# Row sums of layer 2's attention: from a VectorE reduction to TensorE products with a column of ones

## The chip, the cores and the metric

The kernel runs on one core of one Trainium2 chip. The time is device microseconds of one execution; a kernel's time is the median of several executions. The profile is taken from one further execution, and all its times are microseconds from the start of its span unless marked otherwise. The engines are PE (TensorE; PEld are its weight loads), DVE (VectorE), ACT (ScalarE), POOL (GpSimd) and SP (which here only issues DMAs).

## The reference

The network has four layers on a float32 state x of 4 x 512 x 128. Each normalises x, computes an attention-like branch and a feed-forward branch from the result, and adds the product of the first with the silu of the second to x. Layer 0's branch is a selective scan; layers 1 to 3 have attention with 16 heads of 8 dimensions. The change touches the attention of layer 2, which differs from a softmax: the numerator uses rotated q and k, the denominator the plain ones.

```
att_num = exp(einsum('bhqd,bhkd->bhqk', q_rope, k_rope) * scale)
att_den = sum(exp(einsum('bhqd,bhkd->bhqk', q, k) * scale), axis=-1, keepdims=True)
att = att_num / att_den
y = einsum('bhqk,bhkd->bhqd', att, v)
```

So for each of 4 batches and 16 heads there are two 512 x 512 matrices of exponentials. Of the second only the sum over the keys is needed, one number for each query. The feed-forward branch of layer 2 is a mixture of 8 small experts (called moe2 below).

## The kernel before

**Tiling.** `attention(i, ...)` serves layers 1, 2 and 3. The work is cut into 16 groups, a batch and four heads each, and each group into four steps; a step k is one block of 128 rows for the four heads, taken in two halves (m = 0 and 1) of two heads. Layer 2 has 64 steps, one after the other.

**One step of layer 2** (`step`, with `ahead` = 0). For each half PE computes a first-pass product (`first_pass`, through `pair`, L878: two products of 48 x 128 with 48 x 512 in bf16 into a PSUM tile `wide` of 128 x 1024), ACT takes its exponential into `ep` (L980), and DVE sums `ep` over its 512 columns into `den` (L981). Here the queries stand on the partitions and the keys along the columns. Then, for the same half, PE computes a probability product from the rotated q and k, with the keys on the partitions (`probabilities`, L878 again), and ACT takes its exponential into `at` (L1016). Between the second first-pass product and the second probability product stands `behind(k)`: it calls `apply` for step k-1, in which PE multiplies the four heads' `at` with v (L1032): four float32 products of 128 x 32 with 128 x 512, each on its own strip of 32 columns of the array, all into one PSUM bank `py` and added up over the group's four steps.

**The end of a group.** After a group's fourth step ACT copies `py` to `osb` (L1038), and `finish` transposes it in four pieces on PE (L1049), takes the reciprocal of the sums on DVE (L1052) and multiplies (L1053). In layers 1 and 3 the sums come out of the product with v itself: the v tile `vaug` has 32 columns for each head, the first 8 hold v, column SUM = 8 holds ones, the rest zeros. In layer 2 the reciprocal reads `den`.

**Buffers.** `wide` has three PSUM tiles of two banks each, and the bank pools `bank` and `py` one bank each; these are all eight banks. `ep` has two buffers and `at` three. A tile that is written anew waits until all readers of the tile that held its buffer are done.

**The order.** All engines run their instructions in the order in which the program writes them (`tc.manual_schedule`), each engine in its own queue, with semaphores between them. Other work is put in by `Places`: `place()` is called once after the first half and once after the second half of each step and takes the next piece of the queued generators: the projections of the next batch (`project`: products on PE, `cos` and `qkr` for the rotation on POOL and DVE, casts into bf16 parts by `split`), `finish`, the row norms between the layers (`turn`, `post_rows`, `rows_norm`: statistics on DVE, L416 to L419, then a logarithm and an exponential on ACT, L422 and L423), and moe2. The side work on PE shares the one PSUM tile `bank`. In the last four steps of layer 2 the first pass of layer 3 runs too, whose scores DVE reduces (L985).

Of the kernel before, what the change touches and what calls it, by code (L numbers as in the profile page):

```python
# [11 lines left out]
F32 = mybir.dt.float32  # L12
BF16 = mybir.dt.bfloat16
I32 = mybir.dt.int32
AF = mybir.ActivationFunctionType
ALU = mybir.AluOpType
AX = mybir.AxisListType
# [3 lines left out]
P = 128  # L21
B, L, D = 4, 512, 128
# [7 lines left out]
SUM = HD  # L30


PARTS, FAR, SHIFT = 6, 6 * HD, 60
# [195 lines left out]
def kernel(ctx: ExitStack, tc: tile.TileContext, ap: dict):  # L229
    nc = tc.nc  # L230
    act, dve, pool, pe = nc.scalar, nc.vector, nc.gpsimd, nc.tensor
# [7 lines left out]
    def wide():  # L239
        return psum["wide"].tile([P, 2, 512], F32, tag="wide", name="wide")  # L240

    def bank(tag="bank"):
        tag = tag if psum["split"] else "bank"
        return psum["one"].tile([P, 512], F32, tag=tag, name=tag, bufs=psum["bufs"].get(tag, 2))
# [29 lines left out]
    def const(name):  # L274
        at, n = _CST[name]
        return cst[:, at : at + n]

    def col(name, i=0):
        at, _ = _COLS[name]
        return cols[:, at + i : at + i + 1]  # L280

    def row(name, n=4):
        r = _ROWS[name]
        return rows[:, r : r + 1, :].to_broadcast([P, n, D])
# [556 lines left out]
    def attention(i, hp, lp, xnT, pads, vaug, s_io, done=lambda b: None):  # L841
# [16 lines left out]
        if i == 2:  # L858
            kinds = ("q", "k", "qr", "kr")
            rope = lp.tile([P, 2, L], F32, name="rope")  # L860
            nc.sync.dma_start(out=rope, in_=ap["c_rope"])
        if i == 3:
            qbs = hp.tile([P, 1], F32, name="qbs")
            dve.tensor_scalar(qbs, col("q_b"), QSCALE, None, ALU.mult)
# [6 lines left out]
        def pair(lhs, rhs, n, m, blk, lo, hi, rows, own):  # L871


            ps = wide()
            cs = slice(blk * P, (blk + 1) * P)
            for j in range(2):
                r = slice(64 * j, 64 * j + rows)
                pe.matmul(ps[:, j, lo:hi], lhs[m][r, cs], rhs[m][r, lo:hi], start=True, stop=not own)  # L878
            if own:
                h = 4 * groups[n][1] + 2 * m  # L880
                for j in range(2):
                    lhs_own, rhs_own = ident_bf, mask_bf if causal else diag_bf[:, h + j, :]
                    if own == "keys":
                        lhs_own, rhs_own = rhs_own, lhs_own
                    pe.matmul(ps[:, j, cs], lhs_own, rhs_own, start=False, stop=True)  # L885
            return ps
# [34 lines left out]
        def project(b):  # L921

            places.need((i - 1, b))
            ts = slice(b * L, (b + 1) * L)
            w = wide()
            for m in range(2):
                pe.matmul(w[:, m, :], wqk[:, m, :], xnT[:, ts], start=True, stop=True)  # L927
            t = hp.tile([P, 2, L], F32, tag="qk", name="qk")
            if i == 3:
                act.activation(t[:, 0, :], w[:, 0, :], AF.Identity, bias=qbs, scale=QSCALE)  # L930
                act.activation(t[:, 1, :], w[:, 1, :], AF.Identity, bias=col("k_b"))
            else:
                act.activation(t[:, 0, :], w[:, 0, :], AF.Identity, scale=QSCALE)
                act.copy(t[:, 1, :], w[:, 1, :])
            yield 1
            values(b)
            yield 1
            parts = []
            if i == 2:
                cos, sin = (rope[:, m : m + 1, :].to_broadcast([P, 2, L]) for m in range(2))  # L940
                c = lp.tile([P, 2, L], F32, tag="cos", name="cos")
                pool.tensor_tensor(c, t, cos, ALU.mult)
                w = wide()
                for m in range(2):
                    pe.matmul(w[:, m, :], const("rot"), t[:, m, :], start=True, stop=True)
                r = lp.tile([P, 2, L], F32, tag="qkr", name="qkr")
                dve.tensor_tensor(r, w, sin, ALU.mult)
                pool.tensor_tensor(r, r, c, ALU.add)
                parts.append((r, lp.tile([P, 2, PARTS, L], BF16, tag="rparts", name="rparts")))
                yield 1  # L950
            parts.insert(0, (t, hp.tile([P, 2, PARTS, L], BF16, tag="parts", name="parts")))
            dense[b] = {}
            for kk, (_, d) in zip((("q", "k"), ("qr", "kr")), parts):
                dense[b].update({k: d[:, m].rearrange("p s t -> p (s t)") for m, k in enumerate(kk)})
            splits = [split(t, d, b) for t, d in parts]
            for _ in range(3):
                for sp in splits:
                    next(sp)
                yield 0
# [10 lines left out]

        def first_pass(n, qc, m):

            s = st[n]
            hi = (qc + 1) * P if causal else L
            ps = pair(s["q"], s["k"], n, m, qc, 0, hi, SHIFT if i == 3 else FAR, i != 2)
            if i == 2:
                if qc == 0 and m == 0:
                    s["den"] = lp.tile([P, 4, 4], F32, tag="den", name="den", bufs=3)
                e = lp.tile([P, 2, L], F32, tag="ep", name="ep", bufs=2)
                act.activation(e, ps, AF.Exp)  # L980
                dve.tensor_reduce(s["den"][:, qc, 2 * m : 2 * m + 2], e, AX.X, ALU.add)  # L981
            else:
                if qc == 0 and m == 0:
                    s["nm"] = hp.tile([P, 4, 4], F32, tag="nm", name="nm", bufs=2)
                dve.tensor_reduce(s["nm"][:, qc, 2 * m : 2 * m + 2], ps[:, :, :hi], AX.X, ALU.max, negate=True)  # L985
# [38 lines left out]
        def apply(n, kc):  # L1024
            b, g = groups[n]
            s = st[n]
            if kc == 0:
                s["po"] = bank("py")
            lo = kc * P if causal else 0
            a = s.pop(kc)  # L1030
            for j in range(4):
                pe.matmul(  # L1032
                    s["po"][32 * j : 32 * j + 32, lo:], vaug[b % 2][:, kc, 4 * g + j, :], a[:, j, lo:],
                    start=kc == 0, stop=kc == 3,
                )
            if kc == 3:
                s["osb"] = hp.tile([P, L], F32, tag="osb", name="osb", bufs=2)
                act.copy(s["osb"], s["po"])  # L1038

        def finish(n):  # L1040

            b, g = groups[n]
            s = st[n]
            if g == 0:
                outs[b] = hp.tile([P, 4, D], F32, tag="o", name="o")
            o = outs[b]
            pt = bank()
            for c in range(4):
                pe.transpose(pt[:, c * P : (c + 1) * P], s["osb"][:, c * P : (c + 1) * P], ident)  # L1049
            pv4 = pt.rearrange("p (c j r) -> p c j r", c=4, r=32)  # L1050
            rs = hp.tile([P, 4, 4], F32, tag="rs", name="rs", bufs=2)
            dve.reciprocal(rs, s["den"] if i == 2 else pv4[:, :, :, SUM])  # L1052
            dve.tensor_tensor(  # L1053
                o[:, :, g * 32 : (g + 1) * 32].rearrange("p c (j d) -> p c j d", d=HD),
                pv4[:, :, :, :HD],
                rs[:, :, :, None].to_broadcast([P, 4, 4, HD]),
                ALU.mult,
            )
            s.clear()
            yield 1  # L1060
            if g < NG - 1:
                return
            o = outs.pop(b)
            oT = hp.tile([P, L], F32, tag="osb", name="oT", bufs=2)
            transpose_chunks(oT, o, 4)
            yield 1
            pp = bank()
            for c in range(4):
                pe.matmul(pp[:, c * P : (c + 1) * P], oT[:, c * P : (c + 1) * P], wvo[:, 1, :], start=True, stop=True)
            ppv = pp.rearrange("p (c d) -> p c d", d=D)  # L1070
            sb = s_io[:, 4 * b : 4 * b + 4, :]
            dve.tensor_tensor(sb, ppv, row("out_b3") if i == 3 else sb, ALU.add)
            if i == 1:
                pool.tensor_tensor(sb, sb, row("b_proj1"), ALU.add)
            done(b)
            yield 1
# [21 lines left out]
        def behind(k):  # L1098

            if k > 0 and k not in through:  # L1100
                through.add(k)
                apply((k - 1) // 4, (k - 1) % 4)
                if k % 4 == 0:
                    places.job(1, finish(k // 4 - 1))
# [539 lines left out]
    s = keep.tile([P, NC, D], F32, name="s")  # L1644
# [8 lines left out]
    with banks("l1", 3, True, bank=1, py=1), tc.tile_pool(name="heads", bufs=1) as hp:  # L1653
# [34 lines left out]
        with ExitStack() as to3, tc.manual_schedule(engines=engines):  # L1688
# [28 lines left out]
            lp = to3.enter_context(tc.tile_pool(name="attn2", bufs=1))  # L1717
# [77 lines left out]
```

## Time and profile before

| what | us |
|---|---|
| three runs | 1807.21, 1817.28, 1823.47; median 1817.28 |
| the profiled execution | 1814.22, its span 1812.5 |
| PE busy | 1373.3 (76%) |
| DVE busy | 1143.7 (63%) |
| ACT busy | 955.1 (53%) |
| POOL busy | 536.2 (30%) |
| mean granted TensorE clock | 0.828 of full speed |
| first and last start of the reduction L981 | 991.8 and 1376.7 |

The page gives busy times over the whole span, in which four layers with different limits follow one another; the first and last start of L981 bound the stretch of layer 2's attention. A line of a group reads: source line, engine, operation, output<-input with shapes, count | busy us, mean ns of one | idle us of the engine just before them, and what ended it. A line of the waits reads: engine and what waited <- what it waited for: us in total, times, longest. A line of the timeline reads: start, duration, engine, line, operation. A line of the busy times by stage reads: stretch, its length, busy us (and instructions) of the engines, the granted TensorE clock, the DMA share and GB/s. One product in float32 leaves two records on PE, so a set of four v products has eight.

### The profile page before, as it was taken

The numbers are of one execution on the slowest core, as the hardware profiler recorded it, in microseconds if no ns is written. First come the engines' busy times: TensorE is split into PE (matmuls) and PEld (weight loads), VectorE is DVE, ScalarE is ACT, GpSimd is POOL, SyncE is SP. The second block draws the span as 40 slices with busy tenths as digits, with TensorE's granted clock in tenths as the row PEclk, the third lists the DMA queues.
The fourth block names the chain that finished last, engine by engine and source line by source line (L and its number), as shares of the span: only waits on it lengthen the run. The fifth ranks groups of instructions, "written<-read, shape, count | busy, mean of one in ns | idle before, by whom it ended". The sixth has DMA issues, their size and how long they took to land.

```text
span 1812.5 us, 22587 instructions
## 1 busy us (share of the span) xinstructions
PE 1373.3 (76%) x7845; PEld 699.2 (39%) x7845; DVE 1143.7 (63%) x1987; ACT 955.1 (53%) x1302; POOL 536.2 (30%) x513
## 2 busy tenths in 40 slices
PE   4678878788857888999586667776767877788771
PEld 2445445445532336888232222222312322233331
DVE  6467677677766664222466775657658799876422
ACT  3555655555524654223335777777885545354640
POOL 1245354444514652111534221214010101031223
PEclk8689889898857878999677877778868898598985
DMA  4557677576321231441302231220310211112112
GB/s 125 144 160 196 157 211 193 141 209 179 99 56 35 44 101 50 142 158 39 72 18 51 39 51 23 40 31 13 58 24 13 86 27 19 18 31 65 45 44 75
DMA packets 119122, 148.64 MB, mean 82 GB/s; under 512 B 15384, under 2 KB 79968, under 8 KB 117216
## 3 DMA queue, kind: packets, MB, share of 16 engines
q1 hardware_dynamic: 112048, 122.55, 28.7%
q0 software_dynamic: 6960, 24.65, 4.0%
q8 instruction: 62, 1.02, 0.2%
q14 instruction: 52, 0.43, 0.1%
HBM read 113.84 MB, written 16.01 MB: 72 GB/s over the span
## 4 chain that ended last, share of the span: by engine, by line
PE 43%; DVE 20%; ACT 15%; issue 10%; DMA 6%; POOL 3%; SPq 1%; POOLq 0%; DVEq 0%; ACTq 0%
PE wide L878 6%; PE py L1032 6%; PE wide L1313 5%; PE bank L562 5%; ACT at L1016 4%; PE py L573 4%; PE wide L885 3%; DMA rep<-ddd 3%; DVE nm L985 3%; PE py L1293 3%; ACT ep L980 3%; DVE den L981 2%; DVE hs L707 2%; PE wide L927 1%; ACT dA L696 1%
## 5 line engine op out<-in xcount | busy, mean ns | idle before, releaser
L1016 ACT ACTIVATE at<-wide 128x1024 f32<-128x1024 f32 (+3 forms) x384 | 352.5, 923 | 265.1 <-PE wide L885 175.6
L985 DVE TENSOR_REDUCE nm<-wide 128x2 f32<-128x1024 f32 (+3 forms) x256 | 256.8, 1019 | 105.1 <-PE wide L885 88.7
L1032 PE MATMUL py<-at,vaug 128*32 128x512 f32 (+3 forms) x1536 | 235.8, 671 | 11.7 <-POOL at L1020 8.5
L709 POOL TENSOR_TENSOR hc<-hs,C 128x512 f32<-128x512 f32 x128 | 163.2, 1279 | 250.3 <-DVE hs L707 145.1
L981 DVE TENSOR_REDUCE den<-ep 128x2 f32<-128x1024 f32 x128 | 155.5, 1217 | 115.0 <-ACT ep L980 114.3
L878 PE MATMUL wide<-k,q 48*128 48x512 bf16 (+4 forms) x768 | 167.9, 413 | 78.1 <-ACT at L1016 42.3
L562 PE MATMUL bank<-xnT,w 128*128 128x512 f32 x256 | 149.3, 738 | 75.7 <-ACT h L563 56.9
L980 ACT ACTIVATE ep<-wide 128x1024 f32<-128x1024 f32 x128 | 132.7, 1037 | 43.5 <-PE wide L878 33.9
L707 DVE TENSOR_TENSOR_SCAN hs<-dA,dBx 128x512 f32<-128x512 f32 x128 | 154.7, 1209 | 0.6 <-POOL hc L709 0.6
L573 PE MATMUL py<-w,h 128*128 128x128 f32 x1024 | 129.5, 288 | 19.6 <-DVE acc L523 19.6
L573 PEld LDWEIGHTS py<-w,h 128*128 128x128 f32 x1024 | 127.3, 204 | 38.6 <-DVE acc L523 27.9
L885 PE MATMUL wide<-own_bf 128*128 128x128 bf16 x880 | 138.8, 245 | 0.0
L696 ACT ACTIVATE dA<-rep,A 128x512 f32<-128x512 f32 x128 | 87.3, 715 | 97.6 <-DVE hs L707 69.4
L878 PE MATMUL wide<-q,k 63*128 63x512 bf16 (+3 forms) x512 | 101.9, 393 | 40.3 <-DVE nm L985 16.2
L703 DVE TENSOR_TENSOR dBx<-B,rep 128x512 f32<-128x512 f32 x128 | 89.0, 696 | 55.5 <-DMA rep<-ddd 35.8
L562 PEld LDWEIGHTS bank<-xnT,w 128*128 128x128 f32 x256 | 58.0, 237 | 166.6 <-ACT h L563 77.5
L878 PEld LDWEIGHTS <-q 48*128 48x128 bf16 (+1 forms) x768 | 49.8, 96 | 163.1 <-issue 145.3
L1313 PE MATMUL wide<-xT,w 128*128 128x256 f32 x456 | 108.5, 387 | 2.1 <-ACT h L1316 1.5
L1318 DVE TENSOR_TENSOR h<-h,wide 128x512 f32<-128x512 f32 x57 | 39.2, 688 | 110.5 <-ACT h L1316 110.5
L563 ACT ACTIVATE h<-bank,cols 128x512 f32<-128x512 f32 x128 | 84.7, 687 | 42.6 <-PE bank L562 42.2
L885 PEld LDWEIGHTS <-own_bf 128*128 128x128 bf16 x880 | 52.2, 101 | 113.8 <-issue 107.3
L878 PE MATMUL wide<-qr,kr 48*128 48x512 bf16 x256 | 61.3, 452 | 45.3 <-ACT ep L980 40.1
(324 smaller groups left out, 2086.7 us busy)
## 6 DMA issues: line engine op xcount, KB each, us to landing
rep<-ddd SPq DMA_DIRECT2D x256, 256.0 KB
q<-parts SPq DMA_DIRECT2D x192, 48.0 KB
k<-parts SPq DMA_DIRECT2D x192, 48.0 KB
w<-in_f_w_dram SPq DMA_DIRECT2D x18, 256.0 KB
ddd<-dd POOLq DMA_DIRECT2D x8, 512.0 KB
w<-in_f_w_dram SPq DMA_DIRECT2D x32, 128.0 KB
qr<-rparts SPq DMA_DIRECT2D x64, 48.0 KB
kr<-rparts SPq DMA_DIRECT2D x64, 48.0 KB
```

The source lines that it names most:

```text
L562: pe.matmul(ph, w1[:, f * P : (f + 1) * P], self.xnT[:, tb * L : (tb + 1) * L], start=True, stop=True)
L573: pe.matmul(py[:, cs], h[:, f, cs], w2[:, f, :], start=(f == 0), stop=(f == 3))
L707: dve.tensor_tensor_scan(h, st[n]["dA"], st[n]["dBx"], 0.0, ALU.mult, ALU.add)
L709: pool.tensor_tensor(hc, h, batch[tiles[n][0]]["C"], ALU.mult)
L878: pe.matmul(ps[:, j, lo:hi], lhs[m][r, cs], rhs[m][r, lo:hi], start=True, stop=not own)
L885: pe.matmul(ps[:, j, cs], lhs_own, rhs_own, start=False, stop=True)
L980: act.activation(e, ps, AF.Exp)
L981: dve.tensor_reduce(s["den"][:, qc, 2 * m : 2 * m + 2], e, AX.X, ALU.add)
L985: dve.tensor_reduce(s["nm"][:, qc, 2 * m : 2 * m + 2], ps[:, :, :hi], AX.X, ALU.max, negate=True)
L1016: act.activation(a[:, :, lo:], ps[:, :, lo:], AF.Exp)
L1032: pe.matmul(s["po"][32 * j : 32 * j + 32, lo:], vaug[b % 2][:, kc, 4 * g + j, :], a[:, j, lo:], start=kc == 0, stop=kc == 3,)
L1313: pe.matmul(ph[:, g, m * SLOT1 : (m + 1) * SLOT1], wk[:, f + g, m, :], self.x[k], start=True, stop=True)
```

## The change

The first pass of layer 2 swaps the roles of q and k, so the keys stand on the partitions of `ep` and the queries along its columns. The DVE reduction and the tile `den` go. `apply` gets four further products per step after those with v: the stationary operand is `ones`, a 128 x 32 float32 tile that is zero but for a column of ones at SUM + 1 = 9, the moving operand the first-pass exponentials of the same step. They add into the same bank `py`, in which row 9 of each head's 32 thus gathers the denominator over the four steps. `finish` reads the sums from column SUM + 1 of the transposed result. The exponentials live until the next step's `apply`, so `ep` has three buffers in place of two; the rotation's `cos` tile now shares these three buffers under the tag `ep` instead of having its own.

```diff
             rope = lp.tile([P, 2, L], F32, name="rope")
             nc.sync.dma_start(out=rope, in_=ap["c_rope"])
+
+            ones = lp.tile([P, 32], F32, name="ones")
+            dve.memset(ones, 0.0)
+            dve.memset(ones[:, SUM + 1 : SUM + 2], 1.0)
...
-                c = lp.tile([P, 2, L], F32, tag="cos", name="cos")
+                c = lp.tile([P, 2, L], F32, tag="ep", name="cos", bufs=3)
                 pool.tensor_tensor(c, t, cos, ALU.mult)
...
         def first_pass(n, qc, m):
             s = st[n]
             hi = (qc + 1) * P if causal else L
-            ps = pair(s["q"], s["k"], n, m, qc, 0, hi, SHIFT if i == 3 else FAR, i != 2)
             if i == 2:
-                if qc == 0 and m == 0:
-                    s["den"] = lp.tile([P, 4, 4], F32, tag="den", name="den", bufs=3)
-                e = lp.tile([P, 2, L], F32, tag="ep", name="ep", bufs=2)
-                act.activation(e, ps, AF.Exp)
-                dve.tensor_reduce(s["den"][:, qc, 2 * m : 2 * m + 2], e, AX.X, ALU.add)
+                ps = pair(s["k"], s["q"], n, m, qc, 0, L, FAR, False)
+                s["e", qc, m] = lp.tile([P, 2, L], F32, tag="ep", name="ep", bufs=3)
+                act.activation(s["e", qc, m], ps, AF.Exp)
             else:
+                ps = pair(s["q"], s["k"], n, m, qc, 0, hi, SHIFT if i == 3 else FAR, True)
...
             for j in range(4):
                 pe.matmul(
                     s["po"][32 * j : 32 * j + 32, lo:], vaug[b % 2][:, kc, 4 * g + j, :], a[:, j, lo:],
-                    start=kc == 0, stop=kc == 3,
+                    start=kc == 0, stop=kc == 3 and i != 2,
                 )
+            if i == 2:
+                for j in range(4):
+                    pe.matmul(
+                        s["po"][32 * j : 32 * j + 32, :], ones, s["e", kc, j // 2][:, j % 2, :], start=False, stop=kc == 3
+                    )
             if kc == 3:
                 s["osb"] = hp.tile([P, L], F32, tag="osb", name="osb", bufs=2)
                 act.copy(s["osb"], s["po"])
...
-            dve.reciprocal(rs, s["den"] if i == 2 else pv4[:, :, :, SUM])
+            dve.reciprocal(rs, pv4[:, :, :, SUM + (i == 2)])
```

## The prediction

> **What bounds the kernel now.** I read the page's busy table first: no engine fills the span (PE 76%, DVE 63%, ACT 53%), so the answer must come from the stage that the change touches. The groups of instructions place it: the first-pass reduction (L981) runs from 991.8 to 1376.7 us, so layer 2's attention is the stretch 990 to 1378, 64 steps in 388 us, 6.06 us a step. The groups of that stretch and its busy times by stage are next.
>
> ```profile
> L981 DVE TENSOR_REDUCE den<-ep 128x2 f32<-128x1024 f32 x128 | 155.5, 1217 | 115.0 <-ACT ep L980 114.3
> L1016 ACT ACTIVATE at<-wide 128x1024 f32<-128x1024 f32 x128 | 133.4, 1042 | 16.2 <-PE wide L878 15.9
> L1032 PE MATMUL py<-at,vaug 128*32 128x512 f32 x510 | 85.9, 750 | 0.0
> 990.00:1378.00 388.00, 279.69 (x1482) 100.34 (x1484) 265.94 (x438) 296.54 (x355) 80.92 (x53) 0.80 0.22 33
> ```
>
> In the last line (PE, PEld, DVE, ACT, POOL busy, then the granted clock) ACT leads with 296.5 of 388 us and idles 92; PE has 280, at a mean clock of 0.80. The waits of ACT in this stretch say what ends its idle time.
>
> ```profile
> ACT ep L980 <- PE wide L878: 33.9, 23, 7.4
> ACT r_r L422 <- DVE r_ve L419: 22.8, 9, 4.0
> ACT at L1016 <- PE wide L878: 15.9, 21, 1.4
> ACT ep L980 <- DVE den L981: 9.4, 3, 6.0
> ```
>
> The timeline shows an undisturbed step (start, duration) and then a set of v products at the lower clock.
>
> ```profile
> 1301.63 0.39 PE L878 MATMUL wide<-k,q 48*128 48x512 bf16 x2
> 1301.95 1.06 PE L1032 MATMUL py<-at,vaug 128*32 128x512 f32 x8
> 1302.94 0.39 PE L878 MATMUL wide<-qr,kr 48*128 48x512 bf16 x2
> 1303.12 1.11 ACT L980 ACTIVATE ep<-wide 128x1024 f32<-128x1024 f32 x1
> 1304.03 1.12 ACT L1016 ACTIVATE at<-wide 128x1024 f32<-128x1024 f32 x1
> 1304.93 1.13 ACT L980 ACTIVATE ep<-wide 128x1024 f32<-128x1024 f32 x1
> ...
> 1073.34 1.93 PE L1032 MATMUL py<-at,vaug 128*32 128x512 f32 x8
> ```
>
> ACT starts an exponential every 0.905 us (1303.12, 1304.03, 1304.93), so four make a step of 3.62 us; PE needs only about 2 us of it at full clock and waits. So ACT bounds the quiet steps, and the 92 us of holes lift the mean to 6.06. About 33 us of the holes wait on DVE directly. Another 24 us are PE's lateness where PE itself waited for DVE to empty the one PSUM bank that all side work shares: PE's waits on DVE results (L1452, L1460, L1422 and others) add up to 48 us.
>
> **What the change removes.** 128 reductions of 1.217 us, 155.5 us of DVE, which falls from 266 to 110 us in the stretch. Only what somebody waited for counts. (a) ACT waiting for the reduction to free an ep buffer: 9.4 us, all gone. (b) ACT waiting for the row statistics (r_ve), 22.8 us in nine waits. The reductions are queued ahead of them: at 1006.96 one ends, the statistics follow, and ACT gets r_ve at 1009.52. DVE without reductions runs ahead of ACT, but the statistics' own chain of about 2.2 us (four of 0.27 + 0.18, then 0.17), in half of the nine behind a POOL product of 1.28 and an addition of 0.68, remains. I take 15 back; the ends are 6 and 22.8. (c) Of the 24 us behind bank readers, the largest (7.40, ACT resuming at 1092.29) is PE behind the top-2 selection, in whose way two reductions stand and which started behind two more: 4 x 1.22 = 5 back. The 6.53 before 1146.08 is mostly DVE work of its own slowed beside POOL (casts of 1.4 and 1.6 against 0.68): 2.5 back. The waits before 1212.82, 1242.84, 1272.96 and 1110.37 have one or two reductions or statistics each in front: 8.5 back together. That is 16, with ends 5 and 24. Together 40 us, ends 20 and 56.
>
> **What it adds.** Each step gets four products of ones [128 x 32] with ep [128 x 512] in float32: the shapes and the dtype of the v products, on the same four column strips and the same PSUM bank, behind them. The v set starts its second half 0.45 us after the first and ends after 1.06, so a continued set costs 2 x 0.43 = 0.86 us, at the lower clock 1.72 (the set takes 1.93). The trace shows no such continued set. From below it is near nothing, if it filled strips idle during the v products (four strips are already busy, so I don't take it); from above a set by itself, 1.06 or 1.93. I take 0.86 and 1.72. That is 64 x 0.86 to 64 x 1.72, 55 to 110 us of PE, beside 108 idle.
>
> It would be hidden but for **the new wait**. ep has three buffers, and when the second first-pass exponential of step k is written (call it e1), the two of step k-1 and the first of step k are alive. So e1 must wait until the ones products of step k-1 have read theirs, and PE issues these after step k's second first-pass product and the v products. Behind e1 in ACT's queue stand the osb copy, the second probability exponential (a1) and the next step's, and PE's next v products wait for a1. In the step shown the v products end at 1303.01; ones to 1303.87; 0.07 for the signal (the osb copy starts 0.07 after the set that ends at 1281.44); e1 at 1303.94 in place of 1303.12: 0.82 lost, and since all that follows hangs on a1, lost in every such step (3.62 becomes 4.43). Where PE was behind (set 1127.53 to 1128.59, a1 at 1128.95) the ones end at 1129.45, e1 starts at 1129.52, a1 at 1130.43: 1.48. At the lower clock (1073.34 to 1075.27, a1 at 1075.86) a1 comes at 1075.27 + 1.72 + 0.07 + 0.905 = 1077.97: 2.1. I worked this out for all 63 steps from the set's end, with 0.47 for the osb copy where one stands between: 41 sets at full clock give 33 us, 22 at a lower one 45.
>
> Two corrections. Seven full-clock steps cost nothing only because e1 was late by DVE; that cover goes: +6. And eight of the 22 slow sets stand right behind PE pauses that DVE made, which go; PE also gets denser, so I let 12 turn full, at 2 us each: -24. **Price 60**, ends 33 + 6 = 39 and 78 + 6 = 84.
>
> The clock in the profile's rows by 8 us (PE busy, granted clock):
>
> ```profile
> 1056.00:1064.00 8.00, 5.06 (x24) 0.50 0.36 57
> 1304.00:1312.00 8.00, 6.75 (x46) 1.00 0.23 36
> ```
>
> The first follows a PE pause of 3.45 us and holds another of 2.64; the second is quiet steps. So PE's pauses cost a second time.
>
> The Trainium skill's page "TensorE: Matmul & The Clock Gate", Part 1, says that an idle window of about 3.4 us halves PE's clock and that about 3.4 us of sustained work restores it. It speaks for this change. The trace agrees in part: after a pause of 6.66 us a set at 1043.65 took 1.93 and the next, at 1047.56, 1.07; yet the half clock after 1052.92 lasted some 10 us. By the rule alone nearly all 22 would be full, which is the first rival.
>
> The smaller edits: cos now takes an ep buffer in three projections. POOL's two passes (2.35 and 2.36) hold it for some 5 us, in which e1 has one buffer less; it costs 0 where the wait on PE is longer anyway, at most 13 us if each of three costs two steps 2.2 us; I take 2. The role swap in the first pass keeps the shapes (48 x 128 held, 48 x 512 moved, 0.39 us). The reciprocal now reads PSUM behind the transposes that its neighbour L1053 already awaits, on an idle DVE: 0, at worst 16 x 0.24. Two memsets once: under 1. In the last four steps DVE also reduces layer 3's scores (1.22 each) and gets free: -2.
>
> **Sum**: -40 + 60 + 2 - 2 = +20 us. The profiled execution took 1814.22 us around a span of 1812.5; it becomes 1834. The median of the runs shown is 3 us higher, so I predict **1837**, 1.1% slower. About 1% (18 us) is what a measurement of this kernel can tell from no change.
>
> **Rivals.**
> 1. *The relief wins, faster.* PE without DVE's pauses keeps its full clock: then the 22 slow sets cost 0.1 each, the price is 33 + 6 + 2 + 2 = 43, the relief is near its upper end, 53, and some six waits of 1.38 us for half-clock products go as well, 8: -18, 1799. It decides once no more than about three of the 64 sets take over 1.9 us. For it: the quiet stretch at clock 1.00 has the least PE work per step. Against: half-clock stretches also follow ACT's own blocks (five us of table loads and Gelu before 1159.35) and thin products (L463, 3.74 us, then a set of 1.93).
> 2. *They cancel.* Relief 48, price 53: +5, 1822. Nothing in the profile excludes it; both terms are sums of small waits.
> 3. *The wait feeds itself.* e1 waits for PE, PE waits for the buffers that ACT frees, the clock stays low and cos blocks: price 84 + 13, relief 28: +69, 1886.
>
> That the reduction doesn't go is no case: there is no DVE instruction left for it. That e1 doesn't wait could only be if another buffer were free, and four live tiles on three exclude it.
>
> **How the numbers follow.** Forecast 0.42 (own range 1820 to 1862), relief 0.25, cancel 0.23, feeding itself 0.10. Range: the relief's end with 56 and the low price 39 (-17, and 3 for more waits gone) gives 1797; on the other side the high price 84 with relief 20 and 2 for cos less 2 gives +64, 1881; I take 1797 to 1878. Faster by over 1% (below 1799): two thirds of the first rival, 0.17. Within 1%: the rest of it, 0.08, the second, 0.23, and 0.04 of the forecast, 0.35. Slower: 0.48.
>
> **What would show it.** In the changed profile: no den group; L1032's neighbour of 512 records in the stretch with some 0.86 to 1.72 us per set; ACT's waits of ep on PE (ones) as the largest, 40 to 80 us, many of 0.5 to 1.5 us; r_ve down to some 8; steps of 4.4 us in quiet stretches; PE busy 340 or more. It is wrong if quiet steps stay at 3.6 (no wait), if the clock in the stretch is above 0.93 (first rival), or if the projections' steps stall on POOL (third).

## The result, and the profile after

The change made the kernel slightly faster: 1804.49 us (median of 20 runs, 1789.21 to 1816.35) against 1813.84 us for the kernel before (20 runs on the same chip). The ratio of the means, without the one slow run (1816.35 us), is 0.9935 with a 95% interval of 0.9915 to 0.9956. At 1814 us that is 12 us less (8 to 15; the medians themselves lie 9 apart), where 1837 us, 20 more than the median known then, was forecast. The time lies within the range given; the direction was wrong. It falls between two rivals: "they cancel" (+5) and "the relief wins" (-18).

The profiled execution of the changed kernel took 1797.64 us around a span of 1795.9 us, at a mean granted clock of 0.858 (before: 1814.22, 1812.5 and 0.828). From the first to the last start of an ep exponential, layer 2's attention took 384.9 us before and 372.0 us after, 12.9 us less. From there to the end of the span it is 437.1 us, against 436.8 before. The rest of the profile's difference, 4 us, lies ahead of the stage, where the two kernels have the same work. In the kernels run for this study the stage starts anywhere from 981 to 1001 us, so single profiles are compared below by the stage's own length, and kernels by such ratios to the kernel before, timed on the same chip.

The stretch's line in the busy times by stage (window, length, then PE, PEld, DVE, ACT, POOL busy, the granted clock, DMA share, GB/s), after the change:

```profile
986.50:1359.80 373.30, 308.35 (x1976) 109.95 (x1977) 129.84 (x310) 294.08 (x354) 83.47 (x53) 0.92 0.23 34
```

DVE falls from 266 to 130 us, as it had to. PE gets 504 records more (two a product, of 512) and yet only 30 us more busy time; the granted clock of the stage rose from 0.80 to 0.92. ACT's work is unchanged, 294 us, but PE, at 308 of 373 us, is now the busier of the two. The groups of that stretch, after:

```profile
L983 ACT ACTIVATE ep<-wide 128x1024 f32<-128x1024 f32 x128 | 131.5, 1028 | 71.8 <-PE py L1041 56.4 <-POOL qkr L952 9.4 <-PE wide L882 5.5
L1019 ACT ACTIVATE at<-wide 128x1024 f32<-128x1024 f32 x128 | 132.1, 1032 | 0.0
L1035 PE MATMUL py<-at,vaug 128*32 128x512 f32 x504 | 75.0, 670 | 0.0
L1041 PE MATMUL py<-ep,ones 128*32 128x512 f32 x504 | 72.8, 653 | 0.0
```

The v products (L1035) have a mean of 670 ns in place of 750: fewer of them run at the lower clock. Of the 64 sets of v products 11 took over 1.2 us, against 23 before. The ones products (L1041) cost almost as much PE time again. ACT's idle time, 79 us, now stands almost all before the first-pass exponential, as its waits show (total, times, longest):

```profile
ACT ep L983 <- PE py L1041: 56.4, 48, 3.9
ACT ep L983 <- POOL qkr L952: 9.4, 3, 3.2
ACT ep L983 <- PE wide L882: 5.5, 5, 2.3
ACT r_r L422 <- DVE r_ve L419: 1.6, 2, 1.3
```

The new wait is the largest one and is as large as forecast: 56 us in 48 of 63 steps. The old ones are gone: ep behind a late score product from 33.9 to 5.5, the row statistics from 22.8 to 1.6, the probability exponential behind PE from 15.9 to none listed, the reduction from 9.4 to none. So the stage exchanged one set of waits for another and came out ahead. The timeline of a step without other work shows the new wait as it was drawn up (start, duration; idle before and releaser in brackets):

```profile
1266.40 1.06 PE L1035 MATMUL py<-at,vaug 128*32 128x512 f32 x8
1267.28 1.04 PE L1041 MATMUL py<-ep,ones 128*32 128x512 f32 x8
1268.42 1.02 ACT L983 ACTIVATE ep<-wide 128x1024 f32<-128x1024 f32 x1 [1.55 <-PE py L1041]
1269.34 1.02 ACT L1019 ACTIVATE at<-wide 128x1024 f32<-128x1024 f32 x1
```

The ones set starts 0.88 us after the v set and ends at 1268.32; ACT's exponential, which needs the buffer that it reads, starts at 1268.42 after 1.55 us of nothing. Four quiet exponentials now take 4.33 us in place of 3.62.

### The profile page after: what moved, and what is told of

Its sections match the earlier page's. It is cut to its first block, busy times and chain, and to the rows that moved or that the text cites. A ratio compares the mean times of both kernels' runs of the same rounds, so it can differ in the third digit from the quotient of the medians.

```text
span 1795.9 us, 23471 instructions
## 1 busy us (share of the span) xinstructions
PE 1402.4 (78%) x8357; PEld 709.9 (40%) x8357; DVE 1006.8 (56%) x1861; ACT 954.2 (53%) x1302; POOL 538.8 (30%) x513
## 4 chain that ended last, share of the span: by engine, by line
PE 45%; ACT 15%; DVE 14%; issue 10%; DMA 9%; POOL 5%; SPq 2%; POOLq 0%; another core or an unknown queue 0%; ACTq 0%; DVEq 0%
PE py L1035 7%; PE wide L882 6%; PE wide L1321 6%; PE bank L562 5%; ACT at L1019 5%; DMA rep<-ddd 4%; PE py L573 3%; PE wide L889 3%; PE py L1301 3%; ACT ep L983 2%; DVE nm L988 2%; PE py L1041 2%; DVE hs L707 2%; PE wide L931 1%; DMA xs<-acc,pos 1%
## 5 line engine op out<-in xcount | busy, mean ns | idle before, releaser
L1035 PE MATMUL py<-at,vaug 128*32 128x512 f32 (+3 forms) x1536 | 227.0, 646 | 11.6 <-POOL at L1023 8.4
L882 PE MATMUL wide<-q,k 63*128 63x512 bf16 (+4 forms) x768 | 156.6, 395 | 52.2 <-ACT at L1019 32.0
L983 ACT ACTIVATE ep<-wide 128x1024 f32<-128x1024 f32 x128 | 131.5, 1028 | 71.8 <-PE py L1041 56.4
L882 PE MATMUL wide<-k,q 60*128 60x512 bf16 (+4 forms) x512 | 101.8, 383 | 70.6 <-ACT at L1019 34.3
L882 PEld LDWEIGHTS <-k 63*128 63x128 bf16 (+1 forms) x768 | 46.0, 94 | 208.4 <-issue 185.6
L1321 PEld LDWEIGHTS wide<-xT,w 128*128 128x128 f32 x456 | 83.4, 193 | 15.7 <-issue 3.4
L882 PE MATMUL wide<-qr,kr 48*128 48x512 bf16 x256 | 52.5, 402 | 32.0 <-ACT ep L983 29.6
```

What stands on the lines that cost most here:

```text
L983: act.activation(s["e", qc, m], ps, AF.Exp)
L1035: pe.matmul(s["po"][32 * j : 32 * j + 32, lo:], vaug[b % 2][:, kc, 4 * g + j, :], a[:, j, lo:], start=kc == 0, stop=kc == 3 and i != 2,)
L1321: pe.matmul(ph[:, g, m * SLOT1 : (m + 1) * SLOT1], wk[:, f + g, m, :], self.x[k], start=True, stop=True)
```

## The experiments

Two explanations fit a net of -12 us. **Theory A**: the price of the new wait was right (60) and the relief far larger than 40, some 75. **Theory B**: the relief was right and the price far smaller, some 28. A third, **C**, says that neither is a size of its own: relief and price meet in PE's lateness and in its clock. The "stage" below is the length from the first to the last start of an ep exponential in one profiled execution.

**The relief alone.** In the kernel before, the 128 reductions are taken out and a constant stands for the row sums; nothing is added on TensorE. The row sums are left out of the computation.

```diff
                 if qc == 0 and m == 0:
                     s["den"] = lp.tile([P, 4, 4], F32, tag="den", name="den", bufs=3)
+                    dve.memset(s["den"], 512.0)
...
-                dve.tensor_reduce(s["den"][:, qc, 2 * m : 2 * m + 2], e, AX.X, ALU.add)
```

> The kernel before without the 128 reductions (den is set to a constant once a group; the row sums are left out, nothing takes their place, ep keeps two buffers). It measures the relief alone. If the relief was mis-sized (theory A: DVE's queue cost the stage some 75 us, not the 40 of the prediction): 65 to 85 us faster than before, stage of layer 2 near 310 us, ACT's idle time in it near 15 us. If the price of the wait was mis-sized (theory B: the relief is 40 as predicted and the wait costs some 28 net): 35 to 45 us faster, stage near 345. If it is the clock that PE's extra products keep up (theory C): the granted clock of the stage stays near the 0.80 of before and the gain is at most 40; under theory A it rises to 0.88 or more without any added product.

Measured: 1768.87 us against 1813.43, ratio 0.9742 (0.9700 to 0.9783), or -47 us (39 to 54 less). Stage 330.3 us. Busy times of the stretch, and ACT's waits:

```profile
997.00:1328.50 331.50, 263.49 (x1470) 95.93 (x1470) 128.25 (x324) 291.50 (x353) 80.88 (x53) 0.86 0.25 39
```

```profile
ACT ep L981 <- PE wide L878: 17.7, 15, 6.0
ACT at L1016 <- PE wide L878: 9.3, 15, 1.3
ACT r_r L422 <- DVE den L979: 5.1, 1, 5.1
```

The relief is near the value predicted, 40, and within its ends, 20 to 56. A's 75 falls. The time and the clock of 0.86 lie between what was expected under A and under B and C. ACT is busy 291 of 331 us, and its waits for late score products are halved without any change to PE's own work. From here to the changed kernel it is +35 us (0.9742 to 0.9935): that is the price in a stage already relieved of the reductions.

**The price alone.** In the changed kernel the reductions are put back, unused, beside the ones products.

```diff
                 act.activation(s["e", qc, m], ps, AF.Exp)
+                if qc == 0 and m == 0:
+                    s["den"] = lp.tile([P, 4, 4], F32, tag="den", name="den", bufs=3)
+                dve.tensor_reduce(s["den"][:, qc, 2 * m : 2 * m + 2], s["e", qc, m], AX.X, ALU.add)
```

> The changed kernel with the 128 reductions kept beside the ones products (their result is read by nobody; nothing is left out). It measures the price without the relief. Theory A: against the changed kernel 50 to 75 us slower, so some 40 to 65 us slower than before. Theory B: 25 to 35 us slower than before. Theory C: the clock of the stage stays near the changed kernel's 0.92 although DVE is as loaded as before.

Measured: 1881.82 us against 1813.43, ratio 1.0370 (1.0330 to 1.0409), or +67 us (60 to 74). Stage 454.2 us.

```profile
990.00:1445.30 455.30, 340.01 (x1976) 117.06 (x1977) 265.30 (x436) 295.22 (x354) 80.92 (x53) 0.84 0.19 28
```

```profile
ACT ep L983 <- PE py L1044: 101.8, 47, 6.1
ACT r_r L422 <- DVE r_ve L419: 23.8, 9, 3.9
```

Here the price is near the 60 predicted, just above the 40 to 65 expected under A, and B's 28 falls as well. Beside a loaded DVE the same wait, in 47 steps, costs 101.8 us in place of 56.4, and the row statistics are as late as they were before. Removing the reductions is worth 47 us without the ones products and 79 us with them (1.0370 to 0.9935); adding the ones products costs 67 us with the reductions and 35 without. Both differences are 32 us. So the two terms of the sum aren't independent, and neither A nor B is right. Nor is C in the form expected here, that the added products alone hold the clock near 0.92: beside the reductions it is 0.84.

**The order on PE.** In each step the ones products are issued ahead of the v products, which depend on them for nothing but the bank.

```diff
-            for j in range(4):
-                pe.matmul(
-                    s["po"][32 * j : 32 * j + 32, lo:], vaug[b % 2][:, kc, 4 * g + j, :], a[:, j, lo:],
-                    start=kc == 0, stop=kc == 3 and i != 2,
-                )
             if i == 2:
                 for j in range(4):
                     pe.matmul(
-                        s["po"][32 * j : 32 * j + 32, :], ones, s["e", kc, j // 2][:, j % 2, :], start=False, stop=kc == 3
+                        s["po"][32 * j : 32 * j + 32, :], ones, s["e", kc, j // 2][:, j % 2, :], start=kc == 0, stop=False
                     )
+            for j in range(4):
+                pe.matmul(
+                    s["po"][32 * j : 32 * j + 32, lo:], vaug[b % 2][:, kc, 4 * g + j, :], a[:, j, lo:],
+                    start=kc == 0 and i != 2, stop=kc == 3,
+                )
```

> The changed kernel with the ones products issued before the v products of the same step, so that ep is read 0.86 us (full clock) or 1.72 us earlier while PE does the same work. If the wait of ep on the ones products costs the stage what its 56 us in the profile say, this wait falls to some 10 to 20 us, quiet steps go from 4.34 back to 3.6 to 3.8 us, and the time falls by 20 to 40 us against the changed kernel. If the wait only takes the place of holes that would be there anyway, the wait falls but the time by less than 10 us.

Measured: 1786.45 us against 1813.43, ratio 0.9836 (0.9797 to 0.9876), or -30 us. Stage 355.8 us, a quiet step 3.68 us.

```profile
ACT ep L983 <- PE py L1036: 25.3, 27, 3.9
```

The same products, with the same operands, on the same buffers: 18 us of the price came from their place behind the v products. The buffer is free as soon as the ones set ends, and no exponential waits for the v set to end any more. The wait falls from 56.4 to 25.3 us; what is left stands in other steps than the quiet ones. Both figures just miss what was expected, a wait of 10 to 20 us and a gain of 20 to 40.

**cos out of the ep buffers.** In the changed kernel the rotary product gets a tile of its own, worked in two halves so that it fits.

```diff
-                c = lp.tile([P, 2, L], F32, tag="ep", name="cos", bufs=3)
-                pool.tensor_tensor(c, t, cos, ALU.mult)
...
-                r = lp.tile([P, 2, L], F32, tag="qkr", name="qkr")
...
-                pool.tensor_tensor(r, r, c, ALU.add)
+                r = lp.tile([P, 2, L], F32, tag="qkr", name="qkr")
...
+                for m in range(2):
+                    c = lp.tile([P, L], F32, tag="cos", name="cos")
+                    pool.tensor_tensor(c, t[:, m, :], rope[:, 0, :], ALU.mult)
+                    pool.tensor_tensor(r[:, m, :], r[:, m, :], c, ALU.add)
```

> The changed kernel with cos in a small buffer of its own (two halves of 512 columns, one after the other), so that it takes none of the three ep buffers. The wait of ep on POOL (9.4 us in three waits) goes. If these waits stand on the path: 7 to 10 us faster than the changed kernel; if another wait is next (ep on the ones products): less than 4 us.

Measured: 1803.02 us against 1813.43, ratio 0.9944 (0.9915 to 0.9972), the same as the changed kernel within the intervals; stage 372.2 us against 372.0.

```profile
ACT ep L984 <- PE py L1042: 62.5, 46, 6.7
```

The 9.4 us that ACT waited for POOL are gone, and the wait for the ones products is 6.1 us longer. The sharing costs nothing that can be measured: the next wait was right behind it. The run also moves POOL's product behind DVE's, so it isn't the sharing alone.

**PE's time without the wait.** The ones products read a constant tile (`flat`, 128 x 512 ones, written once) in place of ep, so they take PE's time and make nobody wait; ep has two buffers, and cos its own, as in the kernel before. The row sums are left out of the computation.

```diff
-                c = lp.tile([P, 2, L], F32, tag="ep", name="cos", bufs=3)
+                c = lp.tile([P, 2, L], F32, tag="cos", name="cos")
...
-                s["e", qc, m] = lp.tile([P, 2, L], F32, tag="ep", name="ep", bufs=3)
-                act.activation(s["e", qc, m], ps, AF.Exp)
+                e = lp.tile([P, 2, L], F32, tag="ep", name="ep", bufs=2)
+                act.activation(e, ps, AF.Exp)
...
-                        s["po"][32 * j : 32 * j + 32, :], ones, s["e", kc, j // 2][:, j % 2, :], start=False, stop=kc == 3
+                        s["po"][32 * j : 32 * j + 32, :], ones, flat, start=False, stop=kc == 3
```

> The changed kernel in which the ones products read a constant tile of ones in place of the first-pass exponentials (the row sums are left out; every product is still issued, four float32 ones a step at the same place). ep then has no reader and two buffers, cos its own; so DVE is relieved and PE as loaded as in the changed kernel, but no exponential waits for the ones products. It divides the 36 us between the changed kernel and the one without any sums (1804.5 against 1768.9 us). If the price is the wait: within 8 us of 1769, quiet steps at 3.62, no wait of ep on PE's ones. If it is PE's time: 1790 to 1805. The prediction's price was all wait: by it about 1769. Clock of the stage: if the added products warm PE, at or above 0.92; if only the missing DVE pauses do, near the 0.86 of the kernel without sums.

Measured: 1783.29 us against 1813.69, ratio 0.9822 (0.9780 to 0.9863), or -32 us. Stage 348.9 us, quiet steps 3.61 to 3.70.

```profile
995.50:1345.60 350.10, 300.84 (x1962) 107.51 (x1966) 120.41 (x309) 293.92 (x353) 83.29 (x53) 0.92 0.25 37
```

```profile
ACT at L1021 <- PE wide L884: 25.8, 26, 2.6
ACT ep L985 <- PE wide L884: 14.1, 17, 3.4
```

The price of 35 us divides into about 15 for PE's time (0.9742 to 0.9822) and about 20 for the wait (0.9822 to 0.9935); the time lies between the two values expected, so neither is the whole. The time alone isn't free, although PE is idle 49 of 350 us here: score products come later, and ACT's waits for them rise from 27 to 40 us.

**The wait taken away by buffers.** The whole change is kept; ep and cos share five buffers in place of three, and at has two in place of three to make room.

```diff
-                c = lp.tile([P, 2, L], F32, tag="ep", name="cos", bufs=3)
+                c = lp.tile([P, 2, L], F32, tag="ep", name="cos", bufs=5)
...
-                s["e", qc, m] = lp.tile([P, 2, L], F32, tag="ep", name="ep", bufs=3)
+                s["e", qc, m] = lp.tile([P, 2, L], F32, tag="ep", name="ep", bufs=5)
...
-                s[kc] = hp.tile([P, 4, L], F32, tag="at", name="at", bufs=3)
+                s[kc] = hp.tile([P, 4, L], F32, tag="at", name="at", bufs=2)
```

> The changed kernel with five buffers for ep and cos together in place of three (at has two in place of three to make room; nothing is left out). With five, the second first-pass exponential of a step finds a free buffer without the ones products of the step before, also while cos holds one. If the wait is the price: quiet steps back at 3.62, time 1770 to 1780. If it is PE's time: 1790 to 1805, with other waits of ACT on PE in its place.

Measured: 1781.17 us against 1813.69, ratio 0.9811 (0.9765 to 0.9857), or -34 us, the same as with the constant tile and just over the 1770 to 1780 us expected for the wait; stage 345.1 us. The wait for the ones products is gone, and what is left is of the same kind and size as there:

```profile
ACT at L1019 <- PE wide L882: 22.7, 23, 2.6
```

With the row sums right, this shows by another way that the wait is worth some 20 us.

**PE's time without the wait, beside the reductions.** The same constant tile, and the reductions put back.

```diff
-                s["e", qc, m] = lp.tile([P, 2, L], F32, tag="ep", name="ep", bufs=3)
-                act.activation(s["e", qc, m], ps, AF.Exp)
+                e = lp.tile([P, 2, L], F32, tag="ep", name="ep", bufs=2)
+                act.activation(e, ps, AF.Exp)
+                if qc == 0 and m == 0:
+                    s["den"] = hp.tile([P, 4, 4], F32, tag="rs", name="den", bufs=2)
+                dve.tensor_reduce(s["den"][:, qc, 2 * m : 2 * m + 2], e, AX.X, ALU.add)
...
-                        s["po"][32 * j : 32 * j + 32, :], ones, s["e", kc, j // 2][:, j % 2, :], start=False, stop=kc == 3
+                        s["po"][32 * j : 32 * j + 32, :], ones, flat, start=False, stop=kc == 3
```

cos has its own tile here too. The output is divided by the constant tile's sums and the reductions' results go unused, so the row sums are left out again.

> The kernel with the ones products on a constant tile (no exponential waits for them) and the 128 reductions kept on DVE (neither gives the divisor used: the row sums are left out of the result). It divides the 68 us that the ones products cost beside the reductions (1881.8 against 1813.4) into PE's time and the wait. Without reductions PE's time cost 14 us and the wait 21. If PE's time is what grows under DVE's load (PE is late behind DVE, and each set adds to that): 35 to 60 us slower than before. If the wait grows (the products themselves hide in PE's pauses): 5 to 20 us slower than before, and the wait is worth some 50. By the prediction, which charged the wait alone and hid PE's time: no more than 5 us slower.

Measured: 1827.77 us, ratio 1.0143 (1.0111 to 1.0175) to the kernel before on the chip of this run (1801.21 us), or +26 us, between the two ranges expected and well over the 5 us that the prediction allows. The one profile shows a stage of 399.8 us, 15 more than before; but the profile of before is from a run of 1814 us, not 1801, so the stages aren't like for like.

```profile
981.40:1382.30 400.90, 317.37 (x1970) 109.93 (x1970) 264.03 (x436) 295.86 (x353) 80.93 (x53) 0.87 0.21 32
```

```profile
ACT at L1024 <- PE wide L884: 39.6, 30, 3.1
ACT ep L985 <- PE wide L884: 24.5, 21, 7.4
ACT r_r L422 <- DVE r_ve L419: 22.1, 9, 3.5
```

So beside the reductions PE's time costs about 26 us and the wait another 41 (1.0143 to 1.0370), against 15 and 20 without them. By the intervals given I estimate some 10 us of doubt on each such difference: that the wait costs more beside the reductions is just clear of it, that PE's time does is not. The six kernels in one table, in us against the kernel before (ratio less 1, times 1814):

| | no ones products | ones products, no wait | ones products and wait |
|---|---|---|---|
| without reductions | -47 | -32 | -12 (the change) |
| with reductions | 0 (before) | +26 | +67 |

Reading across a row gives the price, down a column the relief. Removing the reductions is worth 47, 58 and 79 us: the more PE has to do and the more ACT waits for it, the more a free DVE is worth.

**Cheaper ones products.** ep and the ones in bfloat16, otherwise as changed; the row sums then add rounded terms.

```diff
-            ones = lp.tile([P, 32], F32, name="ones")
+            ones = lp.tile([P, 32], BF16, name="ones")
...
-                s["e", qc, m] = lp.tile([P, 2, L], F32, tag="ep", name="ep", bufs=3)
+                s["e", qc, m] = lp.tile([P, 2, L], BF16, tag="ep", name="ep", bufs=3)
```

> The changed kernel with ep and ones in bf16 (the exponentials are rounded before they are summed; order and buffers as in the changed kernel). A bf16 product of 512 columns is one pass: pairs of first-pass products start 0.23 us apart at full clock, so the ones set should add about 0.22 us instead of 0.86, and 64 x 0.64 = 41 us less PE time. The wait shrinks by 0.64 us in a quiet step: 3.7 us a step. If wait and PE time are the whole price: 20 to 30 us faster than the changed kernel, near 1780. If ACT's write of bf16 or the weight loads bring something new: less than 10 us faster.

Measured: 1786.76 us against 1813.69, ratio 0.9855 (0.9810 to 0.9901), or -26 us; stage 352.1 us. The ones products' busy time falls from 72.8 to 28 us, and the wait for them from 56.4 to 35.1. That is 15 us under the changed kernel, less than the 20 to 30 expected: a cheaper ones set still stands behind the v set.

```profile
ACT ep L983 <- PE py L1041: 35.1, 28, 3.4
```

**Both, and ep with four buffers.** bfloat16 as above, the ones products first, and the freed memory used for a fourth ep buffer and a cos tile of its own.

```diff
-            ones = lp.tile([P, 32], F32, name="ones")
+            ones = lp.tile([P, 32], BF16, name="ones")
...
-                c = lp.tile([P, 2, L], F32, tag="ep", name="cos", bufs=3)
+                c = lp.tile([P, 2, L], F32, tag="cos", name="cos")
...
-                s["e", qc, m] = lp.tile([P, 2, L], F32, tag="ep", name="ep", bufs=3)
+                s["e", qc, m] = lp.tile([P, 2, L], BF16, tag="ep", name="ep", bufs=4)
...
-                        s["po"][32 * j : 32 * j + 32, :], ones, s["e", kc, j // 2][:, j % 2, :], start=False, stop=kc == 3
+                        s["po"][32 * j : 32 * j + 32, :], ones, s["e", kc, j // 2][:, j % 2, :], start=kc == 0, stop=False
```

The v products follow them, as in the run with the order turned round.

> All three together: ones products first and in bf16, ep with four bf16 buffers, cos with a buffer of its own. No wait of ep on PE, PE time of 0.22 us a step added. It should come to within 10 us of the kernel without sums, 1769 to 1779, and be faster than both kernels of this case. If it stays above 1785, some of the price is neither the wait nor PE's time.

Measured: 1758.71 us against 1813.69, ratio 0.9703 (0.9663 to 0.9743), or -54 us: 3.0% under the kernel before and, by the two ratios, 2.3% under the changed one. It is the fastest kernel here, faster than the 1769 to 1779 us expected, and as fast as the one that computes no row sums at all (0.9742, the intervals overlap). Its stretch, and one set in its timeline:

```profile
993.20:1333.10 339.90, 276.17 (x1720) 102.78 (x1722) 122.99 (x309) 292.43 (x353) 82.57 (x53) 0.86 0.25 38
```

```profile
1256.39 0.40 PE L1036 MATMUL py<-ep,ones 128*32 128x512 bf16 x4
1256.62 1.03 PE L1040 MATMUL py<-at,vaug 128*32 128x512 f32 x8
```

The ones set sets the v products' start back by 0.23 us (a float32 set, in the changed kernel, takes 0.88), nothing waits for it, and the quiet steps are at 3.61 us again, ACT's own pace.

## Why the prediction was wrong, point by point

The sum was -40 + 60 + 2 - 2. Measured along the way from the kernel before to the kernel without sums to the changed one, it is -47 + 35. Of the 32 us between forecast (+20) and result (-12), 7 lie in the relief and 25 in the price. The other way round, by the kernel with reductions and ones products, it is +67 - 79; the change itself makes both steps at once, and only the sum is its own.

- **Relief, (a) to (c), 40.** Right in size: 47, or 55 by the stage in one profile. (a) The 9.4 us behind the reduction went. (b) 22.8 fell to 5.4 without the sums (one wait of 5.1, listed there behind den) and to 1.6 in the changed kernel, where 8 were expected to remain: the statistics' own chain of 2.2 us does run, but early enough. (c) PE's listed waits for DVE in the stage were 48 us before, some 14 without sums and 11 after; ACT's waits for late score products fell by 23 (49.8 to 27.0), where 16 were expected.
- **The wait's mechanism.** Right: three buffers, four live tiles. Quiet steps 4.33 us (4.43 forecast), the ones set 0.88 behind the v set (0.86), 56 us of waits in 48 steps (40 to 80, many of 0.5 to 1.5). PE is busy 308 us, not 340 or more; that forecast failed with the clock, which was set at 0.80 or little above. Beside the reductions, at 0.84, it is 340.
- **Price 60: the step that failed.** It was worked out step by step in the timeline of the kernel *before*, where DVE holds PE late and PE is often at its lower clock. In that setting the sum comes out near, 67 with the reductions in place, but in part by luck: PE's time was put at nothing, as hidden, and there it costs 26 without any wait, which leaves 41 for the wait. And the change doesn't add its wait to that timeline; it adds it to the relieved one, and there the two are 15 and 20, together 35. The correction for this, -24, was the right idea, but it was made for the clock alone. Comparing the kernels step by step, from one probability exponential to its like in the next step, shows where. With the reductions kept, the 41 steps with a full-clock v set lose 35 us (0.86 each) and the 22 with a set at a lower clock 34 (1.55 each). From the kernel without sums to the changed one, 48 full-clock steps lose 32 us (0.66 each) and 15 with a lower-clock set 10 (0.65 each). I had taken 0.81 and 2.0. In the prediction's terms, the full-clock steps were priced at 39 and lost 32, those with a lower-clock set at 45 - 24 = 21 and lost 10: 18 of the 25 us. The other 7 are the distance between these steps of one profile (42) and the ratios (35).
- **Which part of the 60.** The steps with a lower-clock set lost little because 8 of their 15 sets are at full clock in the changed kernel: these 8 steps lost 0.1 us each, the 7 whose sets stay slow 1.3 each. Three sets that were at full clock are slow in the changed kernel, and their steps lost 2.9 each. So 10 steps with a slow set are left, as many as the correction had left (22 less 12), and they lost 18 us together, where the sum had some 21. The 45 steps at full clock in both kernels lost 23 us, 0.51 each, where 41 such steps were priced at 39: that term was mis-sized. Two of the 45 even gained 5 us each. In the kernel without sums ACT waits there 5.1 us for the row statistics and 6.0 us for a late score product; waits as long as these are gone in the changed kernel. In the whole stage ACT idles 40 us without the sums and 79 in the changed kernel, of which 66 are the new waits (56.4 and 9.4) and 13 all others. So 27 us of the new waits stand in place of holes that the relief had left; the sum took the price as coming on top of them.
- **cos sharing, +2.** Nothing measurable. The trace did show its wait (9.4 us), but the run without it shows that the wait behind it takes its place.
- **Layer 3's end, -2.** Not tried by itself; the last four steps take 18.8 us before and 18.7 without the sums, so nothing of it shows.
- **The first rival** (the relief wins, at 18 us below) came nearest, but not by its own condition: it was to decide once no more than three v sets are at half clock, and 8 of the 64 still take over 1.9 us. The clock rose to 0.92, just short of the 0.93 named as its sign. The mechanism, that relief cuts the price too, was in it; it was tied to the clock alone.
- **A reading that no term rests on.** ACT's 92 us of holes don't by themselves lift the step from 3.62 to 6.06 us: 64 quiet steps are 232 of the 388 us, the holes 92, and the other 64 are further work of ACT.

How much of the 32 us of interaction is the clock and how much PE's lateness behind DVE, which the slower clock itself lengthens, no run here separates: each kernel that moves the one moves the other. The runs of the table are from several chips, on which the kernel before took 1813, 1814 and 1801 us, so only the ratios to it are compared.

## What to carry to other kernels

When a change takes a load off one engine and puts a wait on another, don't price the new wait in the old timeline: it lands in the one that the relief leaves, and the two terms add only if nothing waits for both. To find that out, run the two halves alone; the sum of the halves against the whole (here -47 + 67 = +20 against -12) is the size of what the trace of before can't show. And when a late product reads a buffer, look first at its place in its engine's queue: issuing the ones products ahead of the v products was worth 18 us, with no other change.

## What the runs showed of the hardware

**The clock rose with PE's load, from two sides.** In the stage it was granted 0.80 before. Removing DVE's reductions, with PE's work unchanged, gave 0.86 and 16 v sets over 1.2 us in place of 23. Adding the ones products to that gave 0.92 and 11, with the wait (372 us) as without it (349 us), and 0.94 and 10 with five ep buffers. With the cheaper bfloat16 products the clock is back at 0.86 to 0.88, with 18 such sets, and yet those kernels are faster than the changed one. With reductions and ones it is 0.84 to 0.87. So more work on PE partly pays for itself in the clock: from the kernel without sums to the changed one the stage's products take 45 us more, though the ones products alone take 73. And a higher clock is no sign of a faster kernel. The Trainium skill's page "TensorE: Matmul & The Clock Gate", Part 1, says that activity releases the throttle and idle windows bring it back; the runs agree in direction: with DVE's pauses gone the stage's clock rose from 0.80 to 0.86, with the added products to 0.92.

**A second set behind the first.** Four fp32 products of 32 columns behind four of the same shape cost 0.88 us from start to start (1266.40 to 1267.28), against 1.06 for a set seen alone; the ones' weight loads (a group of four takes 0.13 us) lie inside the set before. In bfloat16 a set delays the next by 0.23 us (1256.39 to 1256.62), and ACT writes its exponentials as bfloat16 no faster: 1.03 to 1.05 us in the mean, against 1.03 and 1.04 in float32 (after and before).
